# Cross-attention with 154 keys: two lots of 77 keys, or 128 keys and the remaining 26 of four heads side by side

## The chip, the cores and the metric

The kernel runs on one core of a Trainium2 chip. A core has five engines that run side by side, each in its own order: TensorE (PE; matrix products, with its weight loads listed as PEld), VectorE (DVE), ScalarE (ACT), GpSimd (POOL) and SyncE (SP, which issues most transfers). The on-chip memory (SBUF) has 128 partitions; TensorE writes to a second memory, PSUM, which VectorE and ScalarE can read. The metric is device time in microseconds (us), the median of several runs.

## The reference

Four layers work on x, of 2 batches x 1024 tokens x 288 channels, with a context of 2 x 154 tokens. There are 16 heads of 18 channels. Layers 0 and 1 are blocks of self-attention, cross-attention and a feed-forward part, with linear layers quantised to 8 bits; layers 2 and 3 ("plain" below) are cross-attentions of another kind, over 86 and 68 of the 154 keys separately. The change concerns the cross-attention of layers 0 and 1:

```python
def attn(q, k, v, mask=None):
    logits = jnp.einsum('bqhd,bkhd->bhqk', q, k) / jnp.sqrt(jnp.asarray(q.shape[-1], q.dtype))
    if mask is not None:
        logits = logits + mask
    p = jax.nn.softmax(logits, axis=-1)
    o = jnp.einsum('bhqk,bkhd->bqhd', p, v)
    return o.reshape(o.shape[0], o.shape[1], -1)
...
h = layer_norm(x, ln2_g, ln2_b, 1e-05)
q8, s, sm = quant_act(h)
q = quant_linear(q8, s, sm, wq2, bq2).reshape(b, n, H, D)
t = cond.shape[1]
k = (cond @ wk2.T + bk2).reshape(b, t, H, D)
v = (cond @ wv2.T + bv2).reshape(b, t, H, D)
a = attn(q, k, v, mask[:, None, :, :])
```

Here n is 1024 queries per batch, t is 154 keys, and the mask has 1024 x 154 values per batch, the same for all heads.

## The kernel before

The cross-attention is called four times: for two layers and two batches (`cross_attention`, L1006). Each call first makes its keys and values, and then takes eight steps: two halves of 512 queries, four groups of four heads.

**Keys and values.** The keys lie transposed in a tile kT, with the key's channels (three bf16 parts of each, and rows for the maximum, KM = 120 rows in all) on partitions and the 154 keys side by side for each of 16 heads. POOL writes the constant rows (`head_rows`, L90), the rest goes through `context_key` out to memory and comes back by transfers of SP (`get`, L506). The values stay with their keys on partitions: `context_values` (L998) multiplies the transposed context, 77 keys at a time, by the values' weights in three accumulating products (`matmul3`, L425), and VectorE adds the bias (L1002). A head takes 19 columns: 18 values and a one, so that the product with the weights of the softmax also makes their sum. Before that POOL fills the tile with ones (L1018).

**A step.** The maxima of the logits come first, one step ahead: `cross_maxima` multiplies queries by keys with the queries on partitions (L594), adds the mask (L604) and reduces (L609). The maxima are split into three bf16 parts on POOL (`three`, L188 and L190), transposed on TensorE (L539) and sent by a transfer of ScalarE's queue into rows of the query tile (L549), so that the next product gives logits that are already less their maximum. Then come the products of `attend` (L674). A lot of 77 keys is treated for two heads at a time (`step`): for each head, `weights_unit` (L620) multiplies keys by queries into a PSUM tile of 77 x 512 (L623), VectorE adds the transposed mask and writes it to SBUF (L627), and ScalarE takes the exponential in place (L629). After all four heads of a lot, `strips` (L647, the products at L653) multiplies each head's values by its weights: four products of 32 columns, each into its own strip of 32 partitions of one PSUM tile po. The second lot is accumulated onto the first. At the start of the next step `heads_back` (L660) copies po, transposes it on TensorE (L666) and takes the reciprocal of the sums, and VectorE scales (L711).

With four heads and two lots, a step has eight logit tiles, eight mask adds, eight exponentials and two sets of four strips.

**The mask** is loaded with the queries on partitions and transposed per half in `transpose_mask` (L1033): for each lot four transposes on TensorE (L1038) and a copy by ScalarE (L1043).

**What it shares.** The cross-attention is a generator that runs beside another stream (`beside`, L1403): in the first three calls beside the self-attention, whose reductions (L571), logits and exponentials (L623, L629) and strips (L653) come from the same helpers; in the last beside the plain layers. The streams are woven by weights: each of the four parts of a step yields a weight of 3, and a call of `run` spreads the next step's maxima over the first of them. A scheduler then orders the instructions of each engine. Both streams draw on the same buffers: three PSUM tiles for logits (tag x), two general PSUM tiles (tag mm; po of the cross-attention is one of them), two for the maxima (tag s), three general SBUF rows (row512), and eight SBUF tiles for exponentials (tag e).

In the names of the profile, the digit of the layer is left out, and the letter a stands for self-attention, b for cross-attention and c for feed-forward: bats are logits in PSUM and batse the exponentials of the cross-attention, bato its po, bmT the transposed mask, bcvp and bv the values; aats, aatse, aato and amx belong to the self-attention, and bmx and bmxm to the cross-attention's maxima. An f32 product shows as two records of TensorE.

Of the kernel before, what the change touches and what calls it, by code (L numbers as in the profile page):

```python
# [16 lines left out]
P = 128  # L17
# [6 lines left out]
KC = 96  # L24
TK = 77
NVIP = 68
NTXT = T - NVIP
G = 4
# [24 lines left out]
def tile_xattn(ctx: ExitStack, tc: tile.TileContext, ins: dict, out: bass.AP):  # L53
# [533 lines left out]
    def cross_maxima(qt, g, kt, spans, mask, pool, name):  # L587
# [3 lines left out]
        def unit(c, a):  # L591
            sp = logits(name)
            for j in range(2):
                nc.tensor.matmul(  # L594
                    sp[:, j * T : (j + 1) * T],
                    lhsT=qt[:KR, 2 * a + j, c * P : (c + 1) * P],
                    rhs=kt[:KR, 4 * g + 2 * a + j, :],
                    start=True,
                    stop=True,
                )  # L600
# [18 lines left out]

    def weights_unit(qt, rows, j, keys, kn, maskT, name):  # L620

        sp = ps_x.tile([P, HQ], F32, tag="x", name=name)[:kn]
        nc.tensor.matmul(sp, lhsT=keys(j), rhs=qt[:rows, j, :], start=True, stop=True)  # L623
        e = work.tile([P, HQ], F32, tag="e", name=f"{name}e", bufs=8)[:kn]
        src = sp
        if maskT is not None:
            nc.vector.tensor_tensor(e, sp, maskT, ALU.add)  # L627
            src = e
        nc.scalar.activation(e, src, AF.Exp)  # L629
        return e  # L630
# [42 lines left out]

    def attend(qt, g, key_tiles, a, name, bank=None, eager=False):  # L674

        if bank is None:
            po = ps_o.tile([P, HQ], F32, tag="o", name=f"{name}o")
        else:  # L680
            po = bank(f"{name}o")
        made = {}
# [10 lines left out]
        def step(m, half):  # L693
            keys, kn, v, maskT = key_tiles[m]
            if half == 0:
                if m - 1 in made:
                    weigh(m - 1)
                made[m] = [], v
            for j in (2 * half, 2 * half + 1):
                made[m][0].append(  # L700
                    weights_unit(qt, KM, j, keys, kn, maskT, f"{name}s")
                )
            if half == 1 and eager:
                weigh(m)

        def end():
            if made:
                weigh(len(key_tiles) - 1)
            ptv, rec = heads_back(po, f"{name}o")
            av = a().rearrange("p c (g i d) -> p c g i d", g=G, i=4)  # L710
            nc.vector.tensor_tensor(  # L711
                av[:, :, g, :, :],
                ptv[:, :, :, 0:D],
                rec.unsqueeze(3).to_broadcast([P, HC, 4, D]),
                ALU.mult,
            )
# [6 lines left out]
        return todo, end  # L723

    def attend_pairs(qt, g, keys, vs, zeroed, outs, new, name):

# [4 lines left out]
        def exps(j, n):  # L731
            k0, k1 = ((0, NTXT), (NTXT, T))[n]
            made[j, n] = weights_unit(
                qt, KM, j, lambda j: keys(j)[:, k0:k1], k1 - k0, None, f"{name}s"
            )
# [180 lines left out]
    def self_attention(layers):  # L916
# [20 lines left out]
        for n, (i, g, hf) in enumerate(order):  # L937
# [22 lines left out]
            def products(n=n, i=i, g=g, hf=hf, L=L):  # L960
# [4 lines left out]
                        (  # L965
                            lambda j, m=m: kts[g % 2][: KM, j, m * P : (m + 1) * P],
                            P,
                            L.vt[m],
                            None,
                        )  # L970
# [35 lines left out]
    def cross_attention(w, b, name):  # L1006

        kT = bpool.tile([P, H, T], BF16, tag="kT", name=f"{name}kT")
        head_rows(kT, H, T)
        wk = load_f32(bpool, w["pre"] + "wk2", 1)  # L1010
        krows = new_rows(f"{name}ckr")
        for n in range(3):
            context_key(krows, n, b, [(wk, 0, T)], w["bk"], f"{name}ck")
        get(krows, T, K_PARTS, lambda g: kT[:, 4 * g : 4 * g + 4, :])
        yield 2
        wv = load_f32(bpool, w["pre"] + "wv2", 1)
        v = bpool.tile([TK, 2, VW], F32, tag="v", name=f"{name}v")
        nc.gpsimd.memset(v, 1.0)  # L1018
        for m in range(2):
            context_values(v[:, m, :], TK, b * T + m * TK, wv, w["bv"], f"{name}cv")  # L1020
        yield 2
# [11 lines left out]
        def transpose_mask(hf):  # L1033
            maskTs[hf] = bpool.tile([TK, 2, HQ], F32, tag="maskT", name=f"{name}mT")
            for kc in range(2):
                pt = mm(f"{name}mp")
                for c in range(HC):
                    nc.tensor.transpose(  # L1038
                        pt[:TK, c * P : (c + 1) * P],
                        masks[hf][:, c, kc * TK : (kc + 1) * TK],  # L1040
                        ident,
                    )
                nc.scalar.copy(maskTs[hf][:, kc, :], pt[:TK, :])  # L1043

# [22 lines left out]
        for n in range(2 * G):  # L1067
# [19 lines left out]
            def products(n=n, hf=hf, g=g, out=out):  # L1087
                return attend(
                    qts[n],
                    g,  # L1090
                    [
                        (
                            lambda j, m=m: kT[:KM, 4 * g + j, m * TK : (m + 1) * TK],
                            TK,
                            v[:, m, :],
                            maskTs[hf][:, m, :],
                        )
                        for m in range(2)
                    ],
                    out,  # L1100
                    f"{name}at",
                    mm,
                    True,
                )
# [412 lines left out]
```

## Time and profile before

| | |
|---|---|
| median of 3 runs | 2659.57 us (2655.34 to 2670.14) |
| the profiled execution | 2656.43 us |
| its span, first to last instruction | 2654.5 us, 34216 instructions |
| mean granted clock of TensorE | 0.855 of full speed |
| mask adds of the cross-attention, L627 | 256, 166.6 us busy on VectorE |
| its exponentials, L629 | 256, 155.1 us busy on ScalarE |
| its logits, L623 | 256, 96.7 us busy on TensorE |
| its strips, L653 | 512 records, 73.8 us busy on TensorE |

The profile lists instructions in groups: line, engine, operation, the tile written and the tiles read, shapes and count; then busy time and the mean duration of one; then how long the engine had been idle just before them, and what ended that. The windows view gives, for stretches of the span, the busy time and number of instructions of PE, PEld, DVE, ACT and POOL, then the granted clock, the share of the transfer engines and GB/s. The busy time of TensorE includes the latency of each burst, so that it overstates how full the array is.

### The profile page before, as it was taken

Reading aid. Unit: us, or ns where it says so; the run is one execution under the profiler, and the core shown is the slowest. Engines: PE = TensorE matmul, PEld = TensorE weight load, DVE = VectorE, ACT = ScalarE, POOL = GpSimd, SP = SyncE. Lnnn points to the kernel's source line nnn. Section 1 sums busy time; section 2 is a strip of 40 time slices with the busy share of each in tenths; the row PEclk is TensorE's granted clock in tenths of the full one; section 3 lists DMA queues with packets and bytes.
Section 4 is the critical chain, followed back from the end, with each engine's and each line's share of the span. In section 5 each row is a group of like instructions: output and inputs, shape, how many; then the busy total and the mean of one; then the engine's idle time right before and its main releaser. Section 6 shows DMA issues by size and latency. Waiting matters only on the chain. (4 is left out here: it accounts for less than half of the span.)

```text
span 2654.5 us, 34216 instructions
## 1 busy us (share of the span) xinstructions
PE 2057.5 (78%) x10908; PEld 907.0 (34%) x10908; DVE 1971.1 (74%) x4512; ACT 1409.9 (53%) x2707; POOL 819.3 (31%) x1804
## 2 busy tenths in 40 slices
PE   1488998787884887788768677787767887778898
PEld 0223332323332333233333232323334433444444
DVE  6687888788888477888868958897357876655666
ACT  2346556555664755566656354466654544544443
POOL 7524212402124442022253440123264122413220
PEclk9779888789986888989868778798888977879999
DMA  3422201220000312110023121100033210112321
GB/s 88 122 70 86 57 22 49 77 55 17 27 11 20 119 44 78 42 29 21 6 83 94 31 80 34 33 23 12 25 82 101 74 28 25 51 40 67 86 66 36
DMA packets 158340, 140.27 MB, mean 53 GB/s; under 512 B 44251, under 2 KB 154164, under 8 KB 158161
## 3 DMA queue, kind: packets, MB, share of 16 engines
q1 hardware_dynamic: 147152, 118.67, 15.4%
q0 software_dynamic: 4864, 14.71, 2.3%
q10 hardware_dynamic: 6144, 4.72, 1.0%
q8 instruction: 86, 1.41, 0.2%
q14 instruction: 94, 0.76, 0.1%
HBM read 95.27 MB, written 38.04 MB: 50 GB/s over the span
## 5 line engine op out<-in xcount | busy, mean ns | idle before, releaser
L571 DVE TENSOR_REDUCE L_xattn_amxh<-L_xattn_amx 128x1 f32<-128x512 f32 x1024 | 670.9, 680 | 131.2 <-PE L_xattn_amx L564 123.7
L629 ACT ACTIVATE L_xattn_aatse<-L_xattn_aats 128x512 f32<-128x512 f32 x1024 | 556.1, 600 | 281.2 <-PE L_xattn_aats L623 245.1
L564 PE MATMUL L_xattn_amx<-kT,L_xattn_aqT 108*128 108x512 bf16 x1024 | 425.2, 433 | 122.1 <-DVE L_xattn_amxh L571 91.8
L623 PE MATMUL L_xattn_aats<-L_xattn_aqT,kT 120*128 120x512 bf16 x1024 | 374.7, 413 | 49.8 <-ACT L_xattn_aatse L629 33.4
L653 PE MATMUL L_xattn_aato<-L_xattn_aatse,L_xattn_av 128*32 128x512 f32 x2048 | 288.0, 634 | 22.1 <-ACT L_xattn_aatse L629 18.3
L629 ACT ACTIVATE L_xattn_atse<-L_xattn_ats 86x512 f32<-86x512 f32 (+1 forms) x256 | 139.7, 590 | 121.9 <-PE L_xattn_ats L623 98.5
L623 PEld LDWEIGHTS <-kT 120*128 120x128 bf16 x1024 | 98.9, 103 | 304.3 <-issue 262.0
L564 PEld LDWEIGHTS <-L_xattn_aqT 108*128 108x128 bf16 x1024 | 104.5, 105 | 266.7 <-issue 221.5
L627 DVE TENSOR_TENSOR L_xattn_batse<-L_xattn_bats,L_xattn_bmT 77x512 f32<-77x512 f32 x256 | 166.6, 676 | 37.1 <-PE L_xattn_bats L623 26.5
L629 ACT ACTIVATE L_xattn_batse<-L_xattn_batse 77x512 f32<-77x512 f32 x256 | 155.1, 622 | 37.8 <-DVE L_xattn_batse L627 32.2
L609 DVE TENSOR_REDUCE L_xattn_mxn<-L_xattn_mx 128x2 f32<-128x172 f32 (+1 forms) x512 | 129.3, 304 | 50.4 <-PE L_xattn_mx L594 48.3
L1280 PE MATMUL L_xattn_o<-wo,L_xattn_atp 128*128 128x288 f32 x512 | 143.7, 424 | 4.3 <-ACT L_xattn_mxsr L545 1.8
L604 DVE TENSOR_TENSOR L_xattn_bmxm<-L_xattn_bmx,L_xattn_bm 128x308 f32<-128x308 f32 x256 | 114.6, 464 | 30.8 <-PE L_xattn_bmx L594 25.8
L623 PE MATMUL L_xattn_bats<-L_xattn_bqT,L_xattn_bkT 120*77 120x512 bf16 x256 | 96.7, 433 | 42.0 <-DMA L_xattn_bqT<-L_xattn_bmxsr 29.0
L188 POOL CAST L_xattn_bmxst<-L_xattn_bmxn 128x16 bf16<-128x16 f32 x96 | 20.4, 212 | 345.4 <-DVE L_xattn_bmxn L609 176.2
L623 PE MATMUL L_xattn_ats<-L_xattn_qT,L_xattn_kT 120*86 120x512 bf16 (+1 forms) x256 | 92.5, 422 | 32.0 <-DMA L_xattn_qT<-L_xattn_mxsr 23.5
L609 DVE TENSOR_REDUCE L_xattn_bmxn<-L_xattn_bmxm 128x2 f32<-128x308 f32 x256 | 113.6, 458 | 0.8
L1280 PEld LDWEIGHTS L_xattn_o<-wo,L_xattn_atp 128*128 128x128 f32 x512 | 97.4, 196 | 38.1 <-DVE L_xattn_atp L764 3.6
L594 PE MATMUL L_xattn_mx<-L_xattn_kT,L_xattn_qT 108*128 108x154 bf16 x512 | 79.0, 257 | 26.3 <-DVE L_xattn_mxn L609 11.5
L594 PE MATMUL L_xattn_bmx<-L_xattn_bkT,L_xattn_bqT 108*128 108x154 bf16 x512 | 81.1, 261 | 21.7 <-DVE L_xattn_amxh L571 6.9
L653 PEld LDWEIGHTS L_xattn_aato<-L_xattn_aatse,L_xattn_av 128*32 128x32 f32 x2048 | 41.8, 110 | 155.8 <-ACT L_xattn_aatse L629 129.8
L594 PEld LDWEIGHTS <-L_xattn_bqT 108*128 108x128 bf16 x512 | 49.5, 110 | 99.3 <-issue 69.8
(558 smaller groups left out, 3848.6 us busy)
## 6 DMA issues: line engine op xcount, KB each, us to landing
kT<-L_xattn_akr SPq DMA_DIRECT2D x192, 72.0 KB
L_xattn_aqT<-L_xattn_aqr SPq DMA_DIRECT2D x192, 72.0 KB
L_xattn_bqT<-L_xattn_bqr SPq DMA_DIRECT2D x192, 72.0 KB
L_xattn_qT<-L_xattn_r SPq DMA_DIRECT2D x192, 72.0 KB
L_xattn_akr<-L_xattn_akst SPq DMA_DIRECT2D x16, 324.0 KB
L_xattn_aqr<-L_xattn_aqst SPq DMA_DIRECT2D x16, 324.0 KB
L_xattn_bqr<-L_xattn_bqst SPq DMA_DIRECT2D x16, 324.0 KB
L_xattn_r<-L_xattn_qst SPq DMA_DIRECT2D x16, 324.0 KB
```

What stands on the lines that cost most here:

```text
L188: eng.tensor_copy(part, r)
L564: nc.tensor.matmul(sp, lhsT=qt[:KR, j, c * P : (c + 1) * P], rhs=kt[:KR, j, a * 512 : (a + 1) * 512], start=True, stop=True,)
L571: nc.vector.tensor_reduce(halves[:, a, c, j, :], sp, AX.X, ALU.max, negate=True)
L594: nc.tensor.matmul(sp[:, j * T : (j + 1) * T], lhsT=qt[:KR, 2 * a + j, c * P : (c + 1) * P], rhs=kt[:KR, 4 * g + 2 * a + j, :], start=True ...
L604: nc.vector.tensor_tensor(lm, of, mask[:, c : c + 1, :].to_broadcast([P, 2, T]), ALU.add)
L609: nc.vector.tensor_reduce(nm[:, c, 2 * a : 2 * a + 2, n], of[:, :, k0:k1], AX.X, ALU.max, negate=True,)
L623: nc.tensor.matmul(sp, lhsT=keys(j), rhs=qt[:rows, j, :], start=True, stop=True)
L627: nc.vector.tensor_tensor(e, sp, maskT, ALU.add)
L629: nc.scalar.activation(e, src, AF.Exp)
L653: made = nc.tensor.matmul(po[32 * i : 32 * i + 32, :], lhsT=lhsT, rhs=rhs, start=start, stop=stop)
L1280: nc.tensor.matmul(ps, lhsT=pair[:, c * P : (c + 1) * P], rhs=wo[:, t0 + t, :], start=(t == 0), stop=(t == len(pairs) - 1),)
```

## The change

The 154 keys of a head are divided into 128 and 26 instead of 77 and 77. The first 128 keys of each head make a logit tile of the full 128 partitions. The other 26 of all four heads of a group share one tile: each head has a strip of 32 partitions (26 keys and 6 of padding), written by four products of 32 columns. `attend_context` replaces `attend` here. Its five tiles get their mask adds and exponentials as before. The output is then the sum of two things in po: one product over all 128 partitions of the shared tile, with the values of the 26 keys in a block-diagonal tile `rest` (a head's values stand only in its own rows and its own 32 columns, zeros elsewhere), and the usual four strips for the first 128 keys. The order in the four parts of a step: the shared tile and head 0; head 1; head 2 and the block-diagonal product; head 3 and the strips.

For this the keys' tile gets six columns of padding (TP = 160), cleared by POOL. The values are computed once for 128 keys, and for the other 26 four times, once into each strip of a PSUM tile, from which VectorE adds each head's bias into its block. The mask of the 26 keys is copied four times side by side by POOL into a cleared tile before it is transposed. `attend` and `weights_unit` lose the arguments that only the cross-attention used.

```diff
+TP = 160
...
+    def attend_context(qt, keys, v, rest, maskT, outs, name):
+        po = mm(f"{name}o")
+        es = {}
+
+        def exp(sp, m):
+            e = work.tile([P, HQ], F32, tag="e", name=f"{name}se", bufs=8)
+            nc.vector.tensor_tensor(e, sp, maskT[:, m, :], ALU.add)
+            nc.scalar.activation(e, e, AF.Exp)
+            return e
+
+        def first(j):
+            sp = ps_x.tile([P, HQ], F32, tag="x", name=f"{name}s")
+            nc.tensor.matmul(
+                sp, lhsT=keys(j)[:, 0:P], rhs=qt[:KM, j, :], start=True, stop=True
+            )
+            es[j] = exp(sp, 0)
+
+        def others():
+            sp = ps_x.tile([P, HQ], F32, tag="x", name=f"{name}s")
+            strips(
+                sp, [(keys(j)[:, P:TP], qt[:KM, j, :]) for j in range(4)], True, True
+            )
+            es[4] = exp(sp, 1)
+
+        def weigh_others():
+            nc.tensor.matmul(po, lhsT=rest, rhs=es[4], start=True, stop=False)
+
+        def weigh():
+            strips(po, [(v(j), es[j]) for j in range(4)], False, True)
+
+        def step(n):
+            if n == 0:
+                others()
+            first(n)
+            if n == 2:
+                weigh_others()
+            if n == 3:
+                weigh()
...
-        kT = bpool.tile([P, H, T], BF16, tag="kT", name=f"{name}kT")
-        head_rows(kT, H, T)
+        kT = bpool.tile([P, H, TP], BF16, tag="kT", name=f"{name}kT")
+        head_rows(kT[:, :, 0:T], H, T)
+        nc.gpsimd.memset(kT[:, :, T:TP], 0.0)
...
-        v = bpool.tile([TK, 2, VW], F32, tag="v", name=f"{name}v")
+        v = bpool.tile([P, VW], F32, tag="v", name=f"{name}v")
         nc.gpsimd.memset(v, 1.0)
-        for m in range(2):
-            context_values(v[:, m, :], TK, b * T + m * TK, wv, w["bv"], f"{name}cv")
+        context_values(v, P, b * T, wv, w["bv"], f"{name}cv")
+
+        nr = T - P
+        rest = bpool.tile([P, G, 4, 32], F32, tag="vrest", name=f"{name}vr")
+        nc.gpsimd.memset(rest, 0.0)
+        ps = mm(f"{name}cr")[:, 0:C]
+        for j in range(4):
+            rows_j = slice(32 * j, 32 * j + nr)
+            matmul3(
+                ps[rows_j],
+                lambda k: ctxT[:, k, b * T + P : (b + 1) * T],
+                lambda k: wv[:, k, :],
+            )
+            nc.gpsimd.memset(rest[rows_j, :, j, D : D + 1], 1.0)
+            nc.vector.tensor_tensor(
+                rest[rows_j, :, j, 0:D],
+                ps[rows_j].rearrange("p (g j d) -> p g j d", g=G, j=4)[:, :, j, :],
+                w["bv"][rows_j].rearrange("p (g j d) -> p g j d", g=G, j=4)[:, :, j, :],
+                ALU.add,
+            )
...
+            others = view(row512(f"{name}mo"), c=HC, j=4, k=32)
+            nc.gpsimd.memset(others, 0.0)
+            nc.gpsimd.tensor_copy(
+                others[:, :, :, 0 : T - P],
+                masks[hf][:, :, P:T].unsqueeze(2).to_broadcast([P, HC, 4, T - P]),
+            )
             for kc in range(2):
                 pt = mm(f"{name}mp")
                 for c in range(HC):
                     nc.tensor.transpose(
-                        pt[:TK, c * P : (c + 1) * P],
-                        masks[hf][:, c, kc * TK : (kc + 1) * TK],
+                        pt[:, c * P : (c + 1) * P],
+                        others[:, c].rearrange("p j k -> p (j k)")
+                        if kc
+                        else masks[hf][:, c, 0:P],
                         ident,
                     )
-                nc.scalar.copy(maskTs[hf][:, kc, :], pt[:TK, :])
+                nc.scalar.copy(maskTs[hf][:, kc, :], pt)
```

## The prediction

> **What bounds the kernel now.** The time to beat is the profiled execution: 2656.43 us, of which the trace spans 2654.5 us and about 2 us lie around it. The median of the runs shown is 2659.57, 3.1 us above the profiled one. I read the page's busy shares first, then its 40 slices (DVE and PEclk), because a share over the whole span says little of a kernel whose layers follow each other.
>
> ```profile
> PE 2057.5 (78%) x10908; PEld 907.0 (34%) x10908; DVE 1971.1 (74%) x4512; ACT 1409.9 (53%) x2707; POOL 819.3 (31%) x1804
> ...
> DVE  6687888788888477888868958897357876655666
> ...
> PEclk9779888789986888989868778798888977879999
> ```
>
> No engine is full on average. The changed code runs only in the four cross-attentions (two layers, two batches), so I asked for the logits' exponentials (the tile batse) in slices of 100 us. They lie in four stretches, and the windows view gives the busy time of PE, PEld, DVE, ACT and POOL there:
>
> ```profile
> 520.00:690.00 170.00, 137.74 (x742) 49.20 (x741) 145.49 (x300) 96.34 (x183) 23.42 (x61) 0.89 0.12 33
> 1030.00:1200.00 170.00, 135.60 (x735) 48.99 (x734) 152.12 (x315) 93.35 (x178) 25.77 (x70) 0.90 0.12 33
> 1610.00:1770.00 160.00, 130.99 (x706) 47.40 (x699) 137.45 (x284) 90.48 (x171) 24.28 (x66) 0.87 0.12 33
> 2020.00:2210.00 190.00, 159.62 (x859) 77.64 (x852) 151.37 (x394) 92.98 (x177) 51.71 (x126) 0.83 0.21 57
> ```
>
> In the first three VectorE is the busiest engine, 86 to 89%, with TensorE at 80 to 82% and ScalarE near 56%. In the fourth, beside the plain layers, TensorE leads with 84% against 80%. What the fuller engine waits for is in the waits of VectorE, here from the first stretch (us in total, times, longest):
>
> ```profile
> DVE L_xattn_batse L627 <- PE L_xattn_bats L623: 10.7, 12, 1.9
> DVE L_xattn_amxh L571 <- PE L_xattn_amx L564: 5.7, 11, 1.0
> DVE L_xattn_bmxm L604 <- DMA L_xattn_bm<-in_mask_BxSxS_ff_dram: 4.2, 1, 4.2
> DVE L_xattn_batse L627 <- PE L_xattn_aato L653: 1.5, 2, 1.3
> ```
>
> Only 24.5 us of 170 are idle. The chain of waits is of no help: what it lists in time begins after 1840 us.
>
> **The change, part by part.** Durations come from these groups (count | busy, mean ns | idle before):
>
> ```profile
> L627 DVE TENSOR_TENSOR L_xattn_batse<-L_xattn_bats,L_xattn_bmT 77x512 f32<-77x512 f32 x256 | 166.6, 676 | 37.1 <-PE L_xattn_bats L623 26.5 <-PE L_xattn_aato L653 6.3 <-PE L_xattn_bato L653 2.4
> L629 ACT ACTIVATE L_xattn_batse<-L_xattn_batse 77x512 f32<-77x512 f32 x256 | 155.1, 622 | 37.8 <-DVE L_xattn_batse L627 32.2 <-DVE L_xattn_atT L752 1.7 <-issue 1.2
> ```
>
> 1. Mask adds and exponentials. A step (four heads, 512 queries; 32 steps in all) goes from 8 logit tiles to 5: four of 128 keys, and one holding 26 keys of each head in strips of 32 partitions. That is 256 to 160 of each instruction. Partitions cost nothing: L571 reads 128x512 in 680 ns, the 77x512 add takes 676. VectorE loses 96 x 0.651 (166.6 / 256) = **62.5 us**, ScalarE 96 x 0.606 = 58.2 us. ScalarE has slack, so its part is counted at nothing beyond letting the strips start sooner.
>
> 2. Products in a step. These timeline rows price TensorE (start, us, what; an f32 matmul is two records):
>
> ```profile
> 642.86 1.06 PE L653 MATMUL L_xattn_bato<-L_xattn_batse,L_xattn_bv 77*32 77x512 f32 x8
> 649.60 0.59 PE L623 MATMUL L_xattn_bats<-L_xattn_bqT,L_xattn_bkT 120*77 120x512 bf16 x2 [1.10 <-DMA L_xattn_bqT<-L_xattn_bmxsr]
> 1902.74 5.71 PE L425 MATMUL L_xattn_bcvp<-L_xattn_wv,ctxT 96*77 96x288 f32 x12 [4.20 <-DMA L_xattn_wv<-in_L_xattn_wv_dram]
> ```
>
> A further bf16 matmul of 512 columns costs 0.21 (0.59 for two, 0.38 for one); four f32 strips 1.06; a full-width f32 one 0.86 (six records of the plain queries in 2.58). Before: 8 x 0.21 + 2 x 1.06 = 3.80 us a step. After: 4 x 0.21, the logit strips, one block-diagonal product, four strips. The logit strips are in no row: below, 0.21, all side by side; above, 0.84, one after another. The nearest row, the f32 strips, runs four in 1.06 where one full-width product takes 0.86, so I take 0.21 + 0.20 = 0.41. The block-diagonal product is 0.86. Sum 3.17, so 0.63 less, x 32 = 20 us of TensorE (between 6 and 27).
> [...]
>
> 3. Values. A call had two tiles of 77 keys: 12 records, 3.14 us at 473 us and 5.71 at 1902 (the row above), 0.26 to 0.48 each. Now one tile of 128 keys (6 records) and the 26 others four times over, once for each strip (24): 30 records, 7.9 to 14.3 us, so +4.7 to +8.6 a call, +19 to +34 over four. Neighbouring strips might overlap (down to 9 of 12 matmuls, +12 us). In the program's order the first matmul of each later quarter waits on VectorE, which reads the same bank: three waits a call for a small add. Behind such a wait in TensorE's queue stand the self-attention's products, which VectorE's reductions wait for. I take +6.6 us a call, the middle, 27 in all. From VectorE's side it is alike: its adds at L1002 wait 16.7 us in 8, 2.1 each, and 12 more such waits would be 25. I count half as exposed, **13 us lost**, because around the values (473, 990, 1552, 1902 us; windows of 50) TensorE is 73 to 79% and VectorE 32 to 68% busy, so that other work can fill some of it. The bounds are 0 and 34. The 16 small adds (26x72, between the 0.16 of L576's 128x16 and the 0.45 of L1002), less four adds of 0.45, come to +1.4 us.
>
> 4. Edits that I cost at nothing, with their cover. POOL gets eight clears and eight copies of the mask, clears of the new tiles and of the padding: from L1018 (77x640 in 0.63) and L90 (0.70) some 11 us on an engine that is 31% busy. In the second half the mask copy stands in POOL's queue ahead of the maxima's splits (L188), on which the next logits depend; it waits for the mask's transfer, but so do those maxima. Uncovered it would be 1 us in four places. The mask transposes and their copies keep their number, and so do SP's and ScalarE's DMAs; key rows are still read in pieces of 154 columns.
>
> **The sum.** VectorE has 62.5 - 1.4 = 61 us less to do, 15.3 in each stretch. If its idle time stayed, all of it would come off. In the first three I count 80%, 12.3, because TensorE stands only 4 to 10 points lower and would be 84 to 86% busy in the shortened stretch, where slices of 91% are seen elsewhere. In the fourth I count half, 7.7. 3 x 12.3 + 7.7 = 44.6, less 13 for the values: **-32 us**. 2656.4 - 31.6 = 2625; with the runs' median a little above the profile I say **2626**.
>
> [...] The windows show 0.83 to 0.90 granted here, and the values' matmuls at two rates. [...]
>
> **Rivals.**
> - TensorE is the bound. For it: it waits little, and its products depend on both other engines. Against: its true work (0.21 per matmul) is well below its busy time, which holds the latency of each burst. Then the 20 us of item 2 meet the 19 to 34 of item 3: -1 to +14, 2655 to 2670, about **2663**.
> - The score tiles run out, the slower end. The tiles of tag e have 8 slots for both attentions. The old step gave four back after its second part; the new one holds e0 to e3 to its fourth, where the other attention holds up to four more. An add without a slot stops VectorE with all reductions behind it. The waits on strips (L653) in the third stretch are 2.5 us in three, up to 1.5. If two of the five adds of every step waited out a set of strips, 2 x 1.06 x 32 = 68 us, and 2625 + 68 = **2693**; it turns slower above 1.0 us a step. Against: five tiles a step instead of eight, and such waits are rare now.
>
> **How the numbers follow.** Forecast 0.68 (its own range 2594 to 2650), TensorE 0.17, tiles 0.15. 0.5% of this kernel, 13 us, is about what a measurement can tell from no change. Faster: 0.66 of the forecast and 0.02 of TensorE's case; same: 0.02, 0.13 and 0.03; slower: 0.02 and 0.12. The range 2588 to 2672 leaves out most of the tiles' case and a tail of the forecast in which all 61 us and more come off.
>
> **What would show it.** 160 adds near 0.65 us and 160 exponentials; VectorE's busy time near 1910; the four stretches 8 to 15 us shorter each, with VectorE still above 80% in the first three. Wrong if VectorE's waits for strips grow beyond 30 us, if TensorE's share passes 88% while VectorE's falls, or if the values take over 10 us a call with idle reductions beside them.

## The result, and the profile after

The changed kernel takes 2639.18 us, median of 16 runs (2631.19 to 2655.38), against 2655.40 of the kernel before (16 runs, 2645.21 to 2670.14): a ratio of 0.9942 with a 95% interval of 0.9921 to 0.9962, so about 15 us less where 32 were forecast. The profiled execution of the changed kernel took 2650.96 us (span 2649.2), in the upper part of its runs; its time is not compared with the median.

The page of the changed kernel, busy times first, then slices of VectorE and of the granted TensorE clock:

```profile
PE 2057.4 (78%) x10788; PEld 909.9 (34%) x10788; DVE 1917.7 (72%) x4428; ACT 1359.0 (51%) x2611; POOL 834.2 (31%) x1844
...
DVE  6777887689888486888768938986255786645656
...
PEclk9779878889987898898878768988777887888989
```

VectorE lost 53 us of work, ScalarE 51, and TensorE nothing at all: 2057.5 before, 2057.4 after. The groups say why (count | busy, mean ns | idle before and what ended it), first the two of TensorE before, then those after:

```profile
L623 PE MATMUL L_xattn_bats<-L_xattn_bqT,L_xattn_bkT 120*77 120x512 bf16 x256 | 96.7, 433 | 42.0 <-DMA L_xattn_bqT<-L_xattn_bmxsr 29.0 <-ACT L_xattn_aatse L629 6.8 <-DVE L_xattn_batse L627 3.4
L653 PE MATMUL L_xattn_bato<-L_xattn_batse,L_xattn_bv 77*32 77x512 f32 x512 | 73.8, 650 | 8.0 <-ACT L_xattn_batse L629 5.9 <-DVE L_xattn_bot L436 1.2
```

```profile
L722 DVE TENSOR_TENSOR L_xattn_batse<-L_xattn_bats,L_xattn_bmT 128x512 f32<-128x512 f32 x160 | 107.1, 681 | 23.8 <-PE L_xattn_bats L650 17.1 <-PE L_xattn_bats L728 2.9 <-PE L_xattn_ato L650 1.3
L723 ACT ACTIVATE L_xattn_batse<-L_xattn_batse 128x512 f32<-128x512 f32 x160 | 98.5, 626 | 20.9 <-DVE L_xattn_batse L722 18.7 <-DVE L_xattn_mxn L610 1.2 <-ACT L_xattn_aatse L626 0.4
L728 PE MATMUL L_xattn_bats<-L_xattn_bqT,L_xattn_bkT 120*128 120x512 bf16 x128 | 55.4, 433 | 2.9 <-ACT L_xattn_aatse L626 1.2 <-DVE L_xattn_batse L722 0.7 <-ACT L_xattn_atse L626 0.6
L741 PE MATMUL L_xattn_bato<-L_xattn_batse,L_xattn_bvr 128*128 128x512 f32 x64 | 40.0, 711 | 2.3 <-ACT L_xattn_xT L1324 0.8 <-ACT L_xattn_amxsr L546 0.7 <-ACT L_xattn_mxsr L546 0.4
L426 PE MATMUL L_xattn_bcr<-L_xattn_wv,ctxT 96*26 96x288 f32 x96 | 37.7, 547 | 1.3 <-DVE L_xattn_bvr L1073 1.3
L650 PE MATMUL L_xattn_bato<-L_xattn_batse,L_xattn_bv 128*32 128x512 f32 x256 | 35.8, 630 | 3.9 <-ACT L_xattn_batse L723 3.9
L650 PE MATMUL L_xattn_bats<-L_xattn_bqT,L_xattn_bkT 120*32 120x512 bf16 x128 | 15.0, 457 | 26.4 <-DMA L_xattn_bqT<-L_xattn_bmxsr 26.4
```

The steps do what the change says: 160 adds at 681 ns and 160 exponentials at 626. Logits and weighted sums cost TensorE 55.4 + 15.0 + 40.0 + 35.8 = 146.2 us where they cost 96.7 + 73.8 = 170.5. But the values of the 26 keys, L426 on bcr, cost 37.7 us in 96 records; with bcvp all values together cost 47.5 us against 19.8, which gives all of it back.

The stretches of the steps, from the first to the last step with a finished output (eight steps a call, so seven lengths of a step). The windows view gives length, busy time of PE, PEld, DVE, ACT and POOL, then the granted clock, DMA share and GB/s. Before:

```profile
540.50:686.10 145.60, 116.93 (x636) 42.68 (x634) 125.95 (x265) 83.14 (x159) 22.34 (x56) 0.91 0.12 33
1062.30:1201.30 139.00, 112.03 (x622) 40.19 (x620) 122.54 (x258) 81.39 (x156) 22.73 (x56) 0.93 0.12 34
1622.40:1766.30 143.90, 117.52 (x613) 43.02 (x612) 122.48 (x257) 81.86 (x157) 22.23 (x56) 0.86 0.12 33
2067.80:2212.00 144.20, 122.92 (x651) 57.42 (x653) 117.00 (x308) 74.77 (x141) 33.40 (x84) 0.82 0.15 42
```

After:

```profile
557.20:688.50 131.30, 107.38 (x585) 40.30 (x584) 110.95 (x240) 71.10 (x137) 23.90 (x64) 0.91 0.13 36
1062.20:1187.10 124.90, 104.07 (x574) 40.02 (x571) 107.17 (x231) 69.85 (x134) 23.60 (x62) 0.90 0.14 37
1621.50:1743.40 121.90, 102.65 (x570) 38.69 (x574) 107.85 (x232) 71.50 (x135) 23.84 (x64) 0.91 0.14 39
2071.50:2199.60 128.10, 106.33 (x603) 51.49 (x606) 105.31 (x285) 62.07 (x120) 35.32 (x91) 0.89 0.16 46
```

They are shorter by 14.3, 14.1, 22.0 and 16.1 us, **66.5 together**, more than the 44.6 counted. Look at the start times instead of the lengths: the first stretch begins 16.7 us later than before, the second 0.1 earlier although the first gave 14.3 back, and the fourth 3.7 later. In these two profiled executions, what the steps gain is lost outside the stretches: 66.5 less the 5.3 us by which the span is shorter is **61 us**. Piece by piece, with the values of the four calls in the first four pieces: +16.7 before the first stretch, -2.5, +13.3, +26.5, and +7.1 behind the last one. The last piece holds the same work before and after; its granted clock was 0.87 here and 0.90 before, and it is not counted to the change. One candidate for the others is seen in VectorE's waits (us in total, times, longest):

```profile
DVE L_xattn_amxh L572 <- PE L_xattn_amx L565: 151.9, 166, 7.2
DVE L_xattn_bmxm L605 <- PE L_xattn_bmx L595: 54.6, 31, 11.5
...
DVE L_xattn_bvr L1073 <- PE L_xattn_bcr L426: 33.9, 16, 3.6
...
DVE L_xattn_batse L722 <- PE L_xattn_bats L650: 17.1, 21, 2.8
```

The waits for the values are 33.9 us in 16, and the self-attention's maxima wait 28 us longer than before (123.7). The cross-attention's maxima (bmxm) wait 29 us longer than before (25.8), but the fastest version below has 56.8 us of that wait, so it is not the loss. TensorE itself waits only 2.3 us in all for the adds of the 26 keys (L1073). The waits for strips of the rival with too few tiles (on aato, bato and ato) are about 1 us each.

### The profile page after: what moved, and what is told of

It reads as the page before. It is cut to its first block, busy times and chain, and to the rows that moved or that the text cites. A ratio compares the mean times of both kernels' runs of the same rounds, so it can differ in the third digit from the quotient of the medians.

```text
span 2649.2 us, 33827 instructions
## 1 busy us (share of the span) xinstructions
PE 2057.4 (78%) x10788; PEld 909.9 (34%) x10788; DVE 1917.7 (72%) x4428; ACT 1359.0 (51%) x2611; POOL 834.2 (31%) x1844
## 4 chain that ended last, share of the span: by engine, by line
PE 25%; DVE 9%; ACT 6%; DMA 6%; issue 2%; POOL 1%; SPq 1%; ACTq 0%; DVEq 0%; POOLq 0%
PE L_xattn_o L1344 4%; PE L_xattn_aato L650 2%; DVE L_xattn_amxh L572 2%; PE L_xattn_q L426 2%; PE L_xattn_ato L650 2%; PE L_xattn_ats L624 2%; PE L_xattn_aats L624 2%; ACT L_xattn_aatse L626 2%; DMA L_xattn_qT<-L_xattn_mxsr 2%; DMA L_xattn_bqT<-L_xattn_bmxsr 1%; DMA L_xattn_qT<-L_xattn_r 1%; PE L_xattn_mx L595 1%; PE L_xattn_bcr L426 1%; PE L_xattn_amx L565 1%; DVE L_xattn_mxn L610 1%
## 5 line engine op out<-in xcount | busy, mean ns | idle before, releaser
L565 PE MATMUL L_xattn_amx<-kT,L_xattn_aqT 108*128 108x512 bf16 x1024 | 419.6, 429 | 126.0 <-DVE L_xattn_amxh L572 102.0
L605 DVE TENSOR_TENSOR L_xattn_bmxm<-L_xattn_bmx,L_xattn_bm 128x308 f32<-128x308 f32 x256 | 115.9, 468 | 57.8 <-PE L_xattn_bmx L595 54.6
L722 DVE TENSOR_TENSOR L_xattn_batse<-L_xattn_bats,L_xattn_bmT 128x512 f32<-128x512 f32 x160 | 107.1, 681 | 23.8 <-PE L_xattn_bats L650 17.1
L1344 PEld LDWEIGHTS L_xattn_o<-wo,L_xattn_atp 128*128 128x128 f32 x512 | 98.7, 199 | 37.9 <-DVE L_xattn_atp L805 3.1
L723 ACT ACTIVATE L_xattn_batse<-L_xattn_batse 128x512 f32<-128x512 f32 x160 | 98.5, 626 | 20.9 <-DVE L_xattn_batse L722 18.7
L189 POOL CAST L_xattn_bmxst<-L_xattn_bmxn 128x16 bf16<-128x16 f32 x96 | 20.6, 214 | 277.5 <-DVE L_xattn_bmxn L610 202.1
L546 ACT COPY L_xattn_amxsr<-L_xattn_amxspt 12x512 bf16<-12x512 bf16 x32 | 18.4, 574 | 132.8 <-PE L_xattn_amxspt L540 125.8
```

Source lines behind the costliest of these rows:

```text
L565: nc.tensor.matmul(sp, lhsT=qt[:KR, j, c * P : (c + 1) * P], rhs=kt[:KR, j, a * 512 : (a + 1) * 512], start=True, stop=True,)
L605: nc.vector.tensor_tensor(lm, of, mask[:, c : c + 1, :].to_broadcast([P, 2, T]), ALU.add)
L722: nc.vector.tensor_tensor(e, sp, maskT[:, m, :], ALU.add)
L723: nc.scalar.activation(e, e, AF.Exp)
L1344: nc.tensor.matmul(ps, lhsT=pair[:, c * P : (c + 1) * P], rhs=wo[:, t0 + t, :], start=(t == 0), stop=(t == len(pairs) - 1),)
```

## The experiments

Theory when they began: the gain of the steps is given back where the values of the 26 keys (TensorE's products one strip after another, VectorE's add between them) and the mask are made. Rivals: TensorE's own work there, in whatever order; POOL's small clears at the start; chance of the order in which the scheduler lays the instructions. Ratios are to the kernel before, with 95% intervals; the changed kernel stands at 0.9942.

### What sets the pace in the steps

**The mask added twice** for three of the five tiles, so that VectorE has its 96 adds back:

```diff
             nc.vector.tensor_tensor(e, sp, maskT[:, m, :], ALU.add)
+            if twice:
+                nc.vector.tensor_tensor(e, sp, maskT[:, m, :], ALU.add)
...
-            es[j] = exp(sp, 0)
+            es[j] = exp(sp, 0, j > 0)
```

> The changed kernel with the mask add made twice for three of the five tiles of a step, which puts 96 adds of 0.65 us, 62 us, back on VectorE and nothing on the others. Theory (VectorE sets the pace in the stretches): 45 to 65 us more, about 2695. Rival (TensorE or the latency of a step sets it, and VectorE's share mattered little): 25 us more at most.

Measured: 2683.25 us, 1.0109 (1.0076 to 1.0141). The added group:

```profile
L724 DVE TENSOR_TENSOR L_xattn_batse<-L_xattn_bats,L_xattn_bmT 128x512 f32<-128x512 f32 x96 | 65.1, 679 | 0.2
```

Against the changed kernel that is 1.67% or 44 us for 65.1 us of added work: 0.68 us of time for one of VectorE's.

**The block-diagonal product made twice**, the second over the first:

```diff
-            nc.tensor.matmul(po, lhsT=rest, rhs=es[4], start=True, stop=False)
+            nc.tensor.matmul(po, lhsT=rest, rhs=es[4], start=True, stop=True)
+            nc.tensor.matmul(po, lhsT=rest, rhs=es[4], start=True, stop=False)
```

> The product of the four heads' other keys is made twice into the same bank (the second time over the first), 32 more products of 0.86 to 1.06 us: 28 to 34 us more of TensorE, none of VectorE. If VectorE sets the pace of the steps, as the version with 96 more adds says (44 of 62 us came back), a quarter or less shows: 2639 to 2648. If TensorE has become the bound, 2663 to 2675.

Measured: 2664.95 us, 1.0033 (1.0019 to 1.0047). The added group:

```profile
L742 PE MATMUL L_xattn_bato<-L_xattn_batse,L_xattn_bvr 128*128 128x512 f32 x64 | 35.0, 629 | 0.0
```

By the ratios this is 24 us slower than the changed kernel for 35.0 us of added busy time: 0.69 us for one of TensorE's. That lies in the range written for TensorE as the bound, and I had leaned to the other. With the adds before it, **no engine alone is the bound of the steps: work on either costs about 0.7 of itself.** By an estimate from the intervals of the ratios, that is 0.5 to 0.8 for VectorE and 0.5 to 0.9 for TensorE. In the profiled executions the four stretches are 32 and 24 us longer than the changed kernel's, so most of both lies in the steps. A likely reason is that the two feed each other in turn (maxima, adds, exponentials, strips) and each waits for the other now and then; both edits also lengthen the way from logit to output within one step, and these runs do not tell the load of an engine from that.

### Mask or values

**Without the mask's clear and copy** (`others` is left out, and the first 128 columns are transposed twice):

```diff
-            others = view(row512(f"{name}mo"), c=HC, j=4, k=32)
-            nc.gpsimd.memset(others, 0.0)
-            nc.gpsimd.tensor_copy(
...
-                        others[:, c].rearrange("p j k -> p (j k)")
-                        if kc
-                        else masks[hf][:, c, 0:P],
+                        masks[hf][:, c, 0:P],
```

> The changed kernel without POOL's clearing and fourfold copy of the mask: the shared tile's mask is taken from the first 128 columns of the mask, so the mask of the 26 keys is left out (all of it is zero in these inputs). Theory: TensorE's waits for POOL's copy, 15 us in three places, go, and with them the place of the copy ahead of the maxima's splits: 5 to 12 us less, about 2631. Rivals: the wait is filled by what follows it, no more than 3 us.

Measured: 2648.86 us, 0.9967 (0.995 to 0.9984). Nothing is gained, although TensorE waits 14.9 us in 3 for that copy in the changed kernel. The test is not clean, because the order moved as well (TensorE's stretches for the values took 63.2 us here and 57.7 in the changed kernel), but the two versions that follow agree with it.

**One strip of values** instead of four:

```diff
-        for j in range(4):
+        for j in range(1):
             rows_j = slice(32 * j, 32 * j + nr)
```

> Leaves out three of the four strips of values (rows of heads 1 to 3 of the block-diagonal tile stay zero), so nine of the twelve 26-row products, three bias adds and three ones rows a call; the mask's clear and copy stay. If the values' own work is what was lost (TensorE work and VectorE's waits for it), this comes out where the version without mask copy and with one strip did: 2610 to 2620 us, VectorE's waits for the strips near 7 us in 4, and the first main step back near 156 us. If the mask copy was a part of that gain (only together with the strips), 2622 to 2635. If chance of the order decides, anything within 10 us of 2639.

Measured: 2609.99 us, 0.982 (0.9788 to 0.9853).

**Both left out together:**

> The changed kernel without the mask copy, and with the values of the 26 keys made for one strip of four only (those of the other three heads are left out): the step is the changed one, the preparation nearly that of before. Theory: the loss outside the stretches goes, 15 to 35 us less than the changed kernel, about 2615, that is 40 us below before. Rival 1 (the stretches themselves gain only what is seen net, 16 us): within 6 us of the changed kernel. Rival 2 (chance of order): anywhere within 8 us.

Measured: 2613.31 us, 0.9834 (0.9803 to 0.9864), the same as one strip within the intervals, so leaving out the mask's copy brings nothing here either, and the mask drops out. What is lost, about 30 us, belongs to the three further strips.

### Which part of the values

Seven versions leave nothing out and only make or place the values otherwise.

**Products grouped:** for each third of the channels the four strips follow each other, and the four adds come after all twelve products.

```diff
-            matmul3(
-                ps[rows_j],
...
+        for k in range(3):
+            for j in range(4):
+                nc.tensor.matmul(
+                    ps[32 * j : 32 * j + nr],
+                    lhsT=ctxT[:, k, b * T + P : (b + 1) * T],
+                    rhs=wv[:, k, :],
+                    start=(k == 0),
+                    stop=(k == 2),
+                )
```

> The changed kernel, with the values of the 26 keys made in another order: all twelve products of the four strips first, going round the strips, and the four bias adds of VectorE after them, so that no product waits for an add that reads its bank. Theory (the gain in the four stretches of cross-attention is given back where values and masks are made): VectorE's waits for these products fall from 33.9 us in 16 to about 15, and the time falls by 5 to 15 us, to about 2629. Rival 1 (TensorE's own work there is what costs, in whatever order): no more than 4 us. Rival 2 (what is lost outside the stretches is chance of order and clock): within 6 us either way.

Measured: 2636.09 us, 0.9927 (0.9899 to 0.9955). The waits of the adds fell from 33.9 us in 16 to 7.7 in 4, TensorE's busy time for the strips from 37.7 to 10.9, and the time hardly moved: 3 us where 5 to 15 were expected.

**One pass:** POOL lays the 26 context columns four times side by side, so that one product fills all 128 rows; VectorE writes the ones.

```diff
-    ctxT = const.tile([KC, 3, B * T], F32, name="ctxT")
+    ctxT = const.tile([KC, 3, B * T + TP - T], F32, name="ctxT")
+    nc.vector.memset(ctxT[:, :, B * T :], 0.0)
...
+        cs = view(row512(f"{name}cx")[:KC, 0 : 3 * P], k=3, j=4, t=32)
+        nc.gpsimd.tensor_copy(
+            cs,
+            ctxT[:, :, b * T + P : b * T + TP]
+            .unsqueeze(2)
+            .to_broadcast([KC, 3, 4, TP - P]),
+        )
+        matmul3(
+            ps,
+            lambda k: cs[:, k].rearrange("p j t -> p (j t)"),
+            lambda k: wv[:, k, :],
+        )
...
-            nc.gpsimd.memset(rest[rows_j, :, j, D : D + 1], 1.0)
+            nc.vector.memset(rest[rows_j, :, j, D : D + 1], 1.0)
```

> Nothing left out: POOL lays the 26 context columns four times side by side (one copy of 96 x 384, 0.5 us a call), so one product of 128 rows makes all four strips: 3 matmuls a call instead of 12; the ones rows by VectorE. If the loss of the values lies in the strips' products and VectorE's waits for them, most of the gain of the version with one strip comes with it: 2612 to 2624 us, waits for the strips under 12 us in all. If the loss lies in VectorE's four adds and POOL's clears, 2630 to 2640.

Measured: **2605.03 us, 0.98 (0.9774 to 0.9825)**: 34 us below the changed kernel by the medians, and faster than both kernels.

**Ones on VectorE** with the changed kernel's twelve products:

```diff
-            nc.gpsimd.memset(rest[rows_j, :, j, D : D + 1], 1.0)
+            nc.vector.memset(rest[rows_j, :, j, D : D + 1], 1.0)
```

> Nothing left out: the four clears to one a call go from POOL to VectorE (16 of about 0.2 us, 3 us more of VectorE). If POOL's small clears at the start shift the order there and cost the first 6 us (VectorE's 12-column scaling held 16.8 us beside POOL's 1152-column multiplies), the first main step comes at 149 to 151 us from the first one's own start, as before, and the run is 3 to 6 us below 2639. If the order of the schedule is chance with a size of its own, it may be up to 10 us to either side, and VectorE's waits for the strips stay near 34 us in 16.

Measured: 2647.06 us, 0.9958 (0.9944 to 0.9971). The first main step (the first exponential of the self-attention) came back, 1.7 us before its old place instead of 6.4 after it, and the end did not: a gain at the start can be lost again later.

**Grouped products and ones on VectorE**, the two edits above together:

> Nothing left out: the twelve strip products in the order that runs four strips beside each other (as in the version with the products grouped) and the ones rows on VectorE. TensorE's stretch for the values is then as short as with one pass (21.8 us in the four calls against 57.7, 18.0 with one pass). If that stretch decides, 2605 to 2618 us like one pass. If what one pass brought is the place of other work (the order of the plain layer's stores and loads near 1940 us), which this edit need not move, it stays near 2636 with 12 us or more from the plain layer's first maxima to its first output product (one pass 4.6).

Measured: 2632.67 us, 0.9922 (0.9897 to 0.9947). TensorE's stretch for the values is nearly as short as with one pass, and the time stays with the grouped products.

**One pass, ones on POOL**, the first part of the edit of one pass alone:

> Nothing left out: one pass, but the ones rows stay on POOL. The first main step comes 6 to 7 us late as in every version with those clears on POOL. If that start counts at the end, 2611 to 2613; if it is caught up, as the version with 12 products and the ones on VectorE says, 2603 to 2610. If it is the order that decides and it happens to turn with the clears, up to 2640.

Measured: 2611.58 us, 0.9832 (0.98 to 0.9865). The interval overlaps that of one pass, so what the ones on POOL cost cannot be told.

**One pass, with the twelve products made as well** ahead of it:

```diff
+        for j in range(4):
+            matmul3(
+                ps[32 * j : 32 * j + nr],
+                lambda k: ctxT[:, k, b * T + P : (b + 1) * T],
+                lambda k: wv[:, k, :],
+            )
         matmul3(
             ps,
             lambda k: cs[:, k].rearrange("p j t -> p (j t)"),
```

> The strips' twelve products are made as well, ahead of the one pass that overwrites them, with no VectorE add between them: TensorE's stretch for the values some 9 to 12 us longer a call, 24 to 34 us more of TensorE's busy time in all, no more waits of VectorE's adds. If TensorE's work in order is what the values cost: 2625 to 2640. If it is the back and forth with VectorE's adds alone: 2605 to 2612.

Measured: 2613.09 us, 0.9846 (0.9805 to 0.9886). VectorE's adds still wait 22.4 us in 3 for the products.

**Another weight in the weaving**, everything else as in the changed kernel:

```diff
                 ALU.add,
             )
-        yield 2
+        yield 3
```

> The changed kernel with one number different: the part of a call that makes the values yields a weight of 3 instead of 2 to the weaving of the two streams. Nothing is computed otherwise, the twelve strip products and VectorE's four adds stay as they are, one after the other. In VectorE's queue the last scaling of the self-attention stands again ahead of the plain layer's first maxima, as before the change and with one pass. If what was lost is the place of such instructions (about 9 us near 1960 us, and what follows), with the values' serial products only a part: 2615 to 2628. If the serial products are all of it: 2634 to 2644. If the order is all of it: 2604 to 2614.

Measured: 2635.82 us, 0.9938 (0.9914 to 0.9962), in the range written for the serial products as all of the loss; one pass and strips, which has them too and ends at 2613, speaks against that reading.

The trace shows what these versions did around the fourth call, from the last step of the third stretch to the first of the fourth. In the table, worked out from start times: TensorE's stretches for the values (all four calls, from the first product to the next other instruction behind the last one); in the fourth call the time from the first product of the values to the plain layer's first keys; from the plain layer's first maxima product to the next output product of the self-attention (aomm); and the whole piece.

| version | values, 4 calls | values to keys | maxima to output | whole piece | median |
|---|---|---|---|---|---|
| before | 19.1 | 32.0 | 3.9 | 301.6 | 2655 |
| changed | 57.7 | 44.6 | 13.3 | 328.1 | 2639 |
| weight 3 | 57.8 | 39.4 | 3.9 | 316.5 | 2636 |
| grouped | 21.8 | 37.0 | 13.4 | 324.5 | 2636 |
| grouped, ones on VectorE | 23.5 | 37.9 | 13.3 | 324.1 | 2633 |
| one strip | 20.1 | 38.0 | 12.1 | 323.7 | 2610 |
| one pass and strips | 41.5 | 37.4 | 3.9 | 302.3 | 2613 |
| one pass, ones on POOL | 19.0 | 32.9 | 5.2 | 304.6 | 2612 |
| one pass | 18.0 | 31.7 | 4.6 | 305.9 | 2605 |

The fourth call in the timeline of TensorE (start us, us, what; idle before in brackets), changed kernel:

```profile
1885.67 3.22 PE L426 MATMUL L_xattn_bcvp<-L_xattn_wv,ctxT 96*128 96x288 f32 x6 [4.34 <-DMA L_xattn_wv<-in_L_xattn_wv_dram]
1888.82 3.08 PE L426 MATMUL L_xattn_bcr<-L_xattn_wv,ctxT 96*26 96x288 f32 x6
...
1892.64 3.08 PE L426 MATMUL L_xattn_bcr<-L_xattn_wv,ctxT 96*26 96x288 f32 x6
1896.03 1.64 PE L426 MATMUL L_xattn_bcr<-L_xattn_wv,ctxT 96*26 96x288 f32 x3 [0.32 <-DVE L_xattn_bvr L1073]
...
1899.43 3.08 PE L426 MATMUL L_xattn_bcr<-L_xattn_wv,ctxT 96*26 96x288 f32 x6 [0.33 <-DVE L_xattn_bvr L1073]
```

The version with the products grouped, and the one with one pass:

```profile
1893.02 3.10 PE L1067 MATMUL L_xattn_bcr<-L_xattn_wv,ctxT 96*26 96x288 f32 x24
```

```profile
1874.64 2.29 PE L427 MATMUL L_xattn_bcr<-L_xattn_wv,L_xattn_bcx 96*128 96x288 f32 x6
```

Four strips one after another cost 14 us from 1888.82 on, of which 1.5 are short products of other work; four side by side cost 3.1, and one set of products over 128 rows 2.3 (the first two at a granted clock of 0.50, the last at 0.83 in the ten microseconds around it, 1870 to 1880). While the changed kernel makes them, little else runs. Its windows row for ten of these microseconds (columns as above):

```profile
1890.00:1900.00 10.00, 9.36 (x25) 2.83 (x24) 0.68 (x3) 1.05 (x2) 0.00 (x0) 0.50 0.15 35
```

TensorE is busy for 9.36 us at half its clock, after the 4.34 us that it waited for the weights; VectorE works 0.68 us, ScalarE 1.05, POOL not at all. In the first two calls it is otherwise, and the clock is the larger part of it. TensorE had sat idle for 1.11 us and not at all before their values, and the granted clock over their 11.0 and 11.9 us was 1.00; a strip's six records took 1.64 us. Before the third and the fourth it had sat idle for 4.71 and 4.34 us, the clock was 0.50, and the same six records took 3.08. That the idle time is the reason for the clock is not shown. Products of other work in between cover 2.4 and 4.3 us in the first two calls, 1.8 and 1.5 in the others.

The other loss is one of order. VectorE's queue at the start of the plain layer, changed kernel and one pass:

```profile
1952.07 0.26 DVE L668 RECIPROCAL L_xattn_aatorec<-L_xattn_aatopt 128x16 f32<-128x16 f32 x1
1955.52 0.99 DVE L610 TENSOR_REDUCE L_xattn_mxn<-L_xattn_mx 128x2 f32<-128x172 f32 x4 [3.19 <-PE L_xattn_mx L595]
1956.43 0.45 DVE L699 TENSOR_TENSOR L_xattn_aa<-L_xattn_aatopt,L_xattn_aatorec 128x288 f32<-128x288 f32 x1
```

```profile
1924.46 0.26 DVE L669 RECIPROCAL L_xattn_aatorec<-L_xattn_aatopt 128x16 f32<-128x16 f32 x1
1924.75 0.46 DVE L700 TENSOR_TENSOR L_xattn_aa<-L_xattn_aatopt,L_xattn_aatorec 128x288 f32<-128x288 f32 x1
```

In the changed kernel the scheduler put four maxima of the plain layer ahead of the self-attention's last scaling (L699). They wait 3.19 us for keys still on their way through memory, and L699, which needed nothing more, waits with them; so do the quantisation and the output products behind it, 13.3 us instead of 4.6. The weight of 3 sets this order right again and makes the piece 11.6 us shorter, but the four stretches of its steps are 50.0 us shorter than before where the changed kernel's are 66.5, and by the medians only 3 us are left. (The two profiled executions lie 15 us apart; 12 to 13 of these lie in the last piece, at 0.87 and at 0.90 of the clock.)

What follows. The loss hangs on how the fourfold strips are made: every version whose values come from one pass, or that has one strip only, ends between 2605 and 2613, and every version whose values come from the four strips (the two with added work aside) between 2633 and 2649. It is not TensorE's time for them alone: with one pass and the strips together that time is 23.5 us longer than with one pass, and 8 us show; with the products grouped it is nearly as short as before the change, and 3 to 6 us show. By this count the order around them would be the larger part, but the one order that was set right by itself brought 3, and one strip ends at 2610 with the order at the plain layer still disturbed (12.1) and a piece of 323.7. **How much of the 34 us is time in the queue and how much is order stays open**; order cannot be held fixed here while the products are changed, and grouped products with the weight of 3 were not run.

The versions with the same twelve serial products in another order (weight 3, ones on VectorE) end at 2636 and 2647; that is the size of chance in the order alone, so single differences below some 10 us between these versions, the 3, 6 and 8 above among them, prove nothing by themselves.

## Why the prediction was right, and where it was wrong

1. **Adds and exponentials.** Right: 62.5 us were forecast for the adds, 166.6 - 107.1 = 59.5 went. VectorE's total fell to 1917.7 (forecast: near 1910).
2. **Products of a step.** Forecast 20 us less, measured 170.5 - 146.2 = 24.3. The logit strips took 15.0 / 32 = 0.47 a set (taken: 0.41), the block-diagonal product 40.0 / 32 = 1.25 in busy time, which holds the latency of a burst (taken: 0.86); a second one directly behind it costs 35.0 / 32 = 1.09 (711 and 629 ns a record). Whether strips next to full-width products cost anything of their own cannot be separated in these rows; the sum came out within the 6 to 27 us given, on its upper side.
3. **The share that counts.** The sum took 80% and 50% of VectorE's saving and nothing of TensorE's. Measured slopes are 0.68 and 0.69, so as an estimate: 59.5 x 0.68 + 24.3 x 0.69 = 57 us. One pass, without the loss of the values, is 50 to 53 us faster than before. The forecast of 44.6 was too small, because the 20 us of item 2 were worked out and then left out of the sum.
4. **The values: the step that failed.** "I count half as exposed, 13 us lost, because around the values ... other work can fill some of it." The waits were sized right (12 more at 2.1 = 25 us; measured 33.9 + 9.7 against 16.7, so 27), and so was TensorE's work (+27; 47.5 against 19.8). The exposure was not: making the strips in one pass brought 34 us, the upper bound of the prediction and more than all of those 27. Nor was it a wait of TensorE: it waited 2.3 us for the adds, and VectorE's waits are TensorE's own time for the strips seen from the other side. The mean shares of windows of 50 us said that engines had room (the one for the third call, from 1560 us, begins behind its values, which start at 1556); in calls 3 and 4 little other work ran beside the strips. And a disturbed order reaches further than the wait itself: the 9 us at the plain layer are in no wait for the values, though one strip shows that such a delay need not reach the end. The sign that the prediction had named for this came true: from first to last product the values took 10.6, 12.0, 17.3 and 16.8 us a call.
5. **The granted clock.** The forecast took no loss of clock in the steps, an estimate of its author, and as a whole they have none against before: granted 0.91, 0.90, 0.91, 0.89 against 0.91, 0.93, 0.86, 0.82, lower only in the second. The values in the third and fourth call ran at 0.50, behind idle times of 4.71 and 4.34 us, as those of the fourth call did before (0.53, after 4.20); the upper price of 14.3 us a call was worked out from such rows, the middle was taken.
6. **POOL and the mask, costed at nothing.** Right within what can be measured, although TensorE waits 14.9 us for the copy; without it nothing is gained.

Together: 57 less 34 is 23 us, of which about 15 were measured; the difference of 8 is within the chance of the order. The two errors had opposite signs and so the time, 2639, came near the 2626 forecast: in part by luck. Of the rivals, the tiles did not run out. TensorE as the only bound (2663) did not come either, but its half of the truth, that work on TensorE counts as much as on VectorE, was missing from the forecast.

## What to carry to other kernels

In a kernel woven from two streams, ask of extra work in the preparation what else runs beside it and at which granted clock, call by call in the timeline; the mean share of a window does not tell. Before a pace-setting engine is named, load each candidate with a known amount of work: here both VectorE and TensorE gave 0.7. Where the same rows are needed in several strips, repeat the small operand once and make one full-height product, instead of one product for each strip with a reader between them: here that brought 34 us.

## What was not expected of the hardware

Products of 26 columns into different strips ran side by side where they followed each other directly: 24 records took 3.10 us in the order strip after strip within a third of the channels (products grouped, fourth call, granted clock 0.50). With adds and other work between the strips, as in the changed kernel, each strip's 6 took 3.08 at the same clock. Over all four calls, at clocks that differ from call to call, the 96 records took 10.9 us with the products grouped, 20.6 with each strip's three products together and no add between the strips (one pass and strips), and 37.7 in the changed kernel.

A tiny instruction of VectorE took as long as POOL had a row of large ones. At the start of the changed kernel the scaling of 12 columns, 0.18 us elsewhere, took 16.75, here with POOL's rows beside it:

```profile
61.69 16.75 DVE L372 TENSOR_SCALAR L_xattn_alq<-L_xattn_alqs 128x12 bf16<-128x12 f32 x1
```

```profile
61.49 2.62 POOL L402 TENSOR_TENSOR L_xattn_alh<-L_xattn_alh,L_xattn_ln 128x1152 f32<-128x1152 f32 x1
64.52 5.19 POOL L402 TENSOR_TENSOR L_xattn_alh<-L_xattn_alh,L_xattn_ln 128x1152 f32<-128x1152 f32 x2
70.20 5.19 POOL L402 TENSOR_TENSOR L_xattn_alh<-L_xattn_alh,L_xattn_ln 128x1152 f32<-128x1152 f32 x2
75.77 2.63 POOL L402 TENSOR_TENSOR L_xattn_alh<-L_xattn_alh,L_xattn_ln 128x1152 f32<-128x1152 f32 x1
```

It began 0.2 us after POOL's first multiplication and ended when the sixth was over, at 78.4. Between the six stand small instructions of POOL, and VectorE's did not end in those gaps. Why it lasted so long is not shown. Before the change the same instruction of VectorE ran at 58.34 in 0.18 us, ahead of that row; it began 2.9 to 4.5 us later in the seven versions with the four small clears on POOL and kept its place, 57.5 to 59.4, in those without them. In two of the seven (the mask added twice, the block-diagonal product made twice) the eight instructions of its group took 9.3 us together instead of 18.0, and the first main step came as late, so the length of this wait does not decide the 6 us at the start; and those did not reach the end.
